# A decoder layer on one core: two kinds of transposes move from the matrix engine to VectorE, DRAM and the DMA queue

## The chip, the core and the metric

The kernel runs on one core of a Trainium2 chip. A core has a matrix engine (PE, whose weight loads are shown as PEld), VectorE (DVE), ScalarE (ACT), GpSimd (POOL) and SyncE (SP), which here only issues transfers. Each engine takes its instructions in order. The metric is the device time of one execution in microseconds (us); a time is a median of several runs.

## What is computed

The input is `x` (32 batches of 128 tokens of 128 channels) and an encoder state `ctx_768` (32 batches of 128 tokens of 96 channels). All is float32. Three blocks follow each other, each of them added to `x`:

```python
x = x + linear_attention(layernorm(x))            # 16 heads of 8, sigmoid q and k
x = x + cross_attention(layernorm(x), ctx_768)    # 16 heads of 64, softmax over 128 encoder tokens
x = x + ffn(layernorm(x))                         # shared SwiGLU + one of 8 experts for each token
```

In the last block, `logits = x3 @ gate_w` with `x3 = layernorm(x)`. The expert is the one with the largest logit; its input is `x3` times the sigmoid of that logit.

## The kernel before

**Groups and pairs.** The 32 batches are 8 groups of 4 (`GT`). Cross-attention is cut into 64 steps: for each group two halves of the heads (`s`), and in each half four batches (`b`). The main loop takes two steps at a time; its variable `a` is 0, 2, ... 62. "Pair 12" in this text is the turn with `a = 12`, that is steps 12 and 13. A group takes eight steps, that is four pairs: 8g, 8g+2, 8g+4 and 8g+6.

**A pair, on PE.** `scores` of both steps; `mix` (tiles `avp`) and `project` (`xyp`) of the two steps before; `queries` (`xqp`); `values` (`vp`); `keys` (`xkp`); and `turn`, which transposes the softmax of the first step (`prTa`, `prTb`), then, after another `keys`, that of the second. Between `scores` and `turn` stands a chain over the other engines: `largest` (DVE, tile `nmax`), `exponentials` (ACT, tile `pr`), `divide` (a reciprocal `rs` on DVE, then a multiplication of `pr` on POOL), and then PE may transpose `pr`.

**Banks.** `bank()` hands out four PSUM buffers in turn. A matmul that takes a buffer waits until the matmul four calls before it has been copied out by DVE or ACT. The helpers `pair()` hand out two larger buffers.

**Work beside the pairs.** Other work is written as generators that stop at named places: `attention(g)`, `prologue(g)` (the second layernorm) and `router(g)` (the third layernorm, logits, the choice of the expert, a token's row in the sorted buffer `xsort`). The loop calls `place("M1")` and so on at fixed places of a pair; every generator that waits at this name goes on to its next stop. `begin` starts them: `attention(a // 8 + 2)` at the end of pairs 2, 10, 18 ... (after it the prologue), `router` of the group just finished in the middle of pairs 10, 18, ... 50, and of group 6 in pair 56. So `router(0)` takes its statistics at the end of pair 10, normalizes in pair 12 (`M1`), is transposed by PE there (`P1`, tile `x3Tp`), copied by ACT to `x3T` (`E2`), has its logits in pair 12 (`P2`, tile `lp`), its maxima in pair 14 (`S1`: five small DVE operations, `top` to `oh`), the scaled rows and the counting in pair 14 (`M1`, `P1`, `E1`: `scored`, `cp`, `placed`) and stores its tokens by indirect transfers in pairs 14 and 16 (`M2`).

**The encoder state.** `load_e(g)` loads four batches, token by token (tile `eg`). PE transposes them in `attention`, behind the matmuls of `oep`, and ACT copies them to `eT`, channels first, as `keys` and `values` need them. Group 0 is done by `encoder`.

**Order.** `InTurn` (line 22) wraps an engine, so that its instructions keep the order in which the program calls them. Transfers of SP are not wrapped: the scheduler puts them where it likes. `clear_sorted(g)` fills the rows of `xsort` of one group with zeros, eight transfers of 264 KB (ten for the last group).

All these instructions are issued by line 40, inside `InTurn`; tiles tell them apart. The lines to know are `load_e` 226, `clear_sorted` 317, `transposed` 383, `attention` 405, `prologue` 560, `queries` 593, `router` 707, and the main loop 1207.

Of the kernel before, what the change touches and what calls it, by code (L numbers as in the profile page):

```python
# [10 lines left out]
F32 = mybir.dt.float32  # L11
I32 = mybir.dt.int32
U32 = mybir.dt.uint32
AF = mybir.ActivationFunctionType
ALU = mybir.AluOpType
AX = mybir.AxisListType

P = 128
# [3 lines left out]
class InTurn:  # L22

    def __init__(self, tc, engine):
        self.tc, self.engine, self.on = tc, engine, False
        self.last, self.transfers = None, []

    def __getattr__(self, name):  # L30
        def issue(*operands, **more):
            transfer = name.endswith("dma_start")
            behind = [] if self.last is None else [self.last]
            if not transfer:
                behind += self.transfers
            with ExitStack() as turn:
                if self.on:
                    for one in behind:
                        turn.enter_context(self.tc.issue_after(one.ins))
                made = getattr(self.engine, name)(*operands, **more)  # L40
            if transfer:
                self.transfers.append(made)
            else:
                self.last, self.transfers = made, []
            return made

        return issue
# [3 lines left out]
def kernel(  # L51
# [31 lines left out]
    nc = tc.nc  # L83
    B, S, D = x.shape
    DE = enc.shape[2]
# [7 lines left out]
    GT = 4  # L93
    NG = B // GT
    GW = GT * S
# [4 lines left out]
    QSCALE = 1.0 / float(DH) ** 0.5  # L100
# [3 lines left out]
    dram = ctx.enter_context(  # L104
        tc.tile_pool(name="dram", bufs=1, space=bass.MemoryType.DRAM)
    )
# [94 lines left out]
    pb = second_part.enter_context(tc.tile_pool(name="pb", bufs=3))  # L201
# [19 lines left out]
    bq_c = column(a_bq, "bq_c", nc.scalar)  # L221


    eg_of = {}

    def load_e(g):
        if g < NG:
            t = pe.tile([P, GT, DE], F32, tag="eg", name=f"eg{g}")
            nc.sync.dma_start(
                out=t, in_=enc[g * GT : (g + 1) * GT].rearrange("b s d -> s b d")  # L230
            )
            eg_of[g] = t
# [84 lines left out]
    def clear_sorted(g):  # L317

        n = GT * S
        first = [e * CAP + g * n for e in range(NE)]  # L320
        if g == NG - 1:
            first += range(NE * CAP, NROW, n)
        for r in first:
            ins = nc.sync.dma_start(
                out=xsort[r : r + n].rearrange("(p k) d -> p k d", p=P), in_=zeros
            )
            for put in sorted_by:
                tc.declare_no_dep(ins.ins, put.ins, reason="those rows lie in front")
            cleared_by.append(ins)

    def unordered(ins, done, why):
# [8 lines left out]
    pe_, dve, act_, pool_ = (  # L340
        InTurn(tc, e) for e in (nc.tensor, nc.vector, nc.scalar, nc.gpsimd)
    )

    def moments(name):
        stats = small.tile([P, GT, 6], F32, tag="stats", name=f"st_{name}")
# [37 lines left out]
    def transposed(src, n, rows, name, ps=None, first=0):  # L383

        ps = bank(name) if ps is None else ps
        for t in range(first, first + n):
            pe_.transpose(ps[0:rows, t * P : (t + 1) * P], src[:, t, :], ident)
        return ps

# [13 lines left out]
    def attention(g, fixed=None):  # L405
# [124 lines left out]
        yield "E3"  # L530
        turned = None
        if g not in eT_of:
            eT_of[g] = pe.tile([DE, GW], F32, tag="eT", name=f"eT{g}")
            turned = act_.copy(eT_of[g], ep[0:DE, :])
            load_e(g + 2)
        ob = pa.tile([P, GT, D], F32, tag="ob", name=f"ob{g}")
        made = dve.tensor_tensor(
            ob, op4, bo_a.unsqueeze(1).to_broadcast([P, GT, D]), ALU.add
# [9 lines left out]


    steps = [(g, s, b) for g in range(NG) for s in range(2) for b in range(GT)]  # L550
    eT_of, xnT_of, qk_of, asked = {}, {}, {}, set()

    def encoder(g, evict):

        eT = pe.tile([DE, GW], F32, tag="eT", name=f"eT{g}")
        eT_of[g] = eT
        evict(eT, transposed(eg_of[g], GT, DE, f"eTp{g}")[0:DE, :])
        load_e(g + 2)

    def prologue(g, fixed=None):  # L560

# [28 lines left out]
        evict(t[:, 1, :], kp)  # L590
        qk_of[g, s, j] = t

    def queries(g, s, j):

        cols = slice((4 * s + j) * P, (4 * s + j + 1) * P)
        asked.add((g, s, j))
        qp = bank(f"xqp{g}_{s}_{j}")
        pe_.matmul(qp, lhsT=wq_x[:, cols], rhs=xnT_of[g], start=True, stop=True)
        act_.activation(qk_of[g, s, j][:, 0, :], qp, AF.Copy, scale=QSCALE)


    v_of, sc_of, pr_of, sums_of, prT_of, oT_of = {}, {}, {}, {}, {}, {}
# [104 lines left out]
    def router(g, part=slice(0, GT)):  # L707
# [4 lines left out]
        of = statistics(xg[g], f"c{name}", part)  # L712
        yield "M1"
        x3 = normalized(xg[g], of, pe, f"c{name}", part)
        yield "P1"
        ps = transposed(x3, n, P, f"x3Tp{name}", first=t0)
        yield "E2"
        if t0 == 0:
            x3T[g] = const.tile([P, GW], F32, tag=f"x3T{g}", name=f"x3T{g}")
        xt = x3T[g]  # L720
        act_.copy(xt[:, t0 * S : (t0 + n) * S], ps[:, t0 * S : (t0 + n) * S])
        yield "P2"
        lp = bank(f"lp{name}")
        for t in range(n):
            pe_.matmul(
# [3 lines left out]
                start=True,  # L729
                stop=True,  # L730
            )
        yield "E3"
        lg = lp[:, 0 : n * NE].rearrange("p (t e) -> p t e", e=NE)
        if n == GT:
            lg = small.tile([P, n, NE], F32, tag="lg", name=f"lg{name}")
# [393 lines left out]
    def place(*which):  # L1129
        for at in which:  # L1130
            for one in list(beside):
                if one[0] == at:
                    one[0] = next(one[1], None)
                    if one[0] is None:
                        beside.remove(one)
                        if one[2] is not None:
                            begin(one[2]())

    for engine in (pe_, dve, act_, pool_):
        engine.on = True

    def whole(g):
# [62 lines left out]
    for a in range(0, n, 2):  # L1207
        both = (a, a + 1)
        scores(a)
        scores(a + 1)  # L1210
        largest(a)
        place("S1")
        if a:
            mix(a - 2)
            mix(a - 1)
        place("S3")
        largest(a + 1)
        exponentials(a)
        for k in both:
            if k + GT < n and steps[k + GT] not in asked:  # L1220
                queries(*steps[k + GT])
        place("M1")
        divide(a)
        if a:
            project(a - 2)
            project(a - 1)

            if a % 8 == 2 and 2 < a < n - 8 or a == n - 8:
                begin(router(steps[a - 1 if a == n - 8 else a - 3][0]))
        for k in both:  # L1230
            if k not in v_of:
                values(k)
        side["now"] = 0
        place("P1")
        if a >= n - 4:
            within["pair"] = 0
            products()
        exponentials(a + 1)
        place("E1")
        divide(a + 1)  # L1240
        place("E2")
        if a == n - 2:
            next(begun[0][1])
        if a == 0:
            for k in (GT + 2, GT + 3):
                queries(*steps[k])
        for k in both:
            if k + GT + 2 < n and steps[k + GT + 2] not in qk_of:
                keys(*steps[k + GT + 2], act_.copy)
            if k == a:  # L1250
                turn(a)
        if a == 0:
            values(2)
        if a == n - 2:
            early = router(NG - 1, slice(0, GT // 2))
            next(early)
            next(early)
        place("S2", "M2")
        side["now"] = 1
        place("P2")  # L1260
        if a >= n - 6:
            within["pair"] = 1
            products()
        place("E3")
        if a == n - 2:
            next(begun[1][1])
            finish()
        while begun and a < n - 2:
            finish()
        turn(a + 1)  # L1270
        if a == 0:
            place("S1")
        if a % 8 == 2:
            clear_sorted(a // 8)
            g = a // 8 + 2
            if g < NG:
                begin(attention(g), lambda g=g: prologue(g))
        if a == 12:
            load_ffn()
        if a == n - 8:  # L1280

            first_part.close()
            pools["g"] = ctx.enter_context(tc.tile_pool(name="pg", bufs=2, side="right"))
            pools["c"] = ctx.enter_context(tc.tile_pool(name="pc", bufs=4, side="right"))
            pd = ctx.enter_context(tc.tile_pool(name="pd", bufs=1, side="right"))
            pools["down"] = pd.tile([P, NE, NC, D], F32, tag="wdr", name="wdr")
            for c in range(NC):
                nc.sync.dma_start(
                    out=pools["down"][:, :, c],
                    in_=rt_down[:, c * P : (c + 1) * P, :].rearrange("e p d -> p e d"),  # L1290
                )
            whole_experts(pd, "up", rt_up)

            pieces += [
                (g, down(g) if c is None else hidden(g, c))
                for g, c in (
                    (0, 0), (0, 1), (1, 0), (1, 1), (2, 0), (2, 1), (0, None),
                    (3, 0), (3, 1), (1, None), (2, None), (3, None),
                )
            ]  # L1300
# [198 lines left out]
```

## Time and profile before

| what | us |
|---|---|
| median of nine runs (lowest, highest) | 621.21 (617.5, 626.33) |
| the profiled execution, its own time | 624.3 |
| its span in the profile | 622.5 |
| PE busy, 4681 matmuls | 598.5 |
| DVE busy | 430.9 |
| ACT busy | 390.3 |
| POOL busy | 248.3 |
| 256 transposes of the softmax's first halves (`prTa`) | 39.2 |
| 28 + 4 transposes of the encoder state (`oep<-ident,eg`, `eTp`) | 4.2 + 0.6 |
| 32 transposes for the router (`x3Tp`) | 5.2 |

The span begins with the first instruction and ends with the last; the execution's own time has 1.8 us more around it. Matmuls are pipelined, so their durations overlap: what one costs PE is the step from its start to the next start, which the timeline shows. The granted clock of the matrix engine is 0.994 over the span. The DMA engines are busy in the first 75 us (loads, and the 66 transfers of `clear_sorted`), and little after that.

### The profile page before, as it was taken

Reading aid. Unit: us, or ns where it says so; the run is one execution under the profiler, and the core shown is the slowest. Engines: PE = TensorE matmul, PEld = TensorE weight load, DVE = VectorE, ACT = ScalarE, POOL = GpSimd, SP = SyncE. Lnnn points to the kernel's source line nnn. Section 1 sums busy time; section 2 is a strip of 40 time slices with the busy share of each in tenths; the row PEclk is TensorE's granted clock in tenths of the full one; section 3 lists DMA queues with packets and bytes.
Section 4 is the critical chain, followed back from the end, with each engine's and each line's share of the span. In section 5 each row is a group of like instructions: output and inputs, shape, how many; then the busy total and the mean of one; then the engine's idle time right before and its main releaser. Section 6 shows DMA issues by size and latency. Waiting matters only on the chain. (4 is left out here: it accounts for less than half of the span.)

```text
span 622.5 us, 13294 instructions
## 1 busy us (share of the span) xinstructions
PE 598.5 (96%) x4681; PEld 451.2 (72%) x4681; DVE 430.9 (69%) x1226; ACT 390.3 (63%) x1414; POOL 248.3 (40%) x248
## 2 busy tenths in 40 slices
PE   8998999999999999999999999999999999997887
PEld 6556777777777777777777767777767766987845
DVE  5747667877786778677867786778657678655435
ACT  4376776776668667766766677677766771544411
POOL 3123423433443444344434453344345344255540
PEclk9989999999999999999999999999999999999989
DMA  6999900000000000000000000013000002342146
GB/s 167 317 363 351 320 2 2 14 2 1 19 14 1 5 28 2 0 12 22 1 2 10 10 2 1 10 57 89 2 10 10 2 9 90 88 109 67 40 117 180
DMA packets 42659, 39.64 MB, mean 64 GB/s; under 512 B 8592, under 2 KB 32656, under 8 KB 42592
## 3 DMA queue, kind: packets, MB, share of 16 engines
q1 hardware_dynamic: 39168, 33.80, 17.7%
q0 software_dynamic: 2144, 4.46, 2.2%
q8 instruction: 38, 0.62, 0.4%
q10 hardware_dynamic: 1280, 0.53, 0.3%
q14 instruction: 29, 0.24, 0.1%
HBM read 14.37 MB, written 24.40 MB: 62 GB/s over the span
## 5 line engine op out<-in xcount | busy, mean ns | idle before, releaser
L40 ACT ACTIVATE pr<-sc,nmax 128x128 f32<-128x128 f32 x512 | 180.5, 387 | 47.7 <-DVE nmax L40 44.9
L40 POOL TENSOR_TENSOR pr<-pr,rs 128x1024 f32<-128x1024 f32 x64 | 121.2, 1897 | 149.3 <-DVE x L40 89.7
L40 ACT ACTIVATION_READ_ACCUMULATOR pr<-sc,nmax 128x1 f32 x512 | 115.8, 226 | 0.0
L40 DVE TENSOR_REDUCE nmax<-sc 128x8 f32<-128x1024 f32 x64 | 78.0, 1220 | 15.2 <-PE sc L40 14.8
L40 PEld LDWEIGHTS xyp<-wo_x,oT 128*128 128x128 f32 x512 | 61.9, 192 | 14.1 <-issue 12.2
L40 PE MATMUL sc<-qk 64*128 64x128 f32 x1024 | 66.0, 279 | 0.7 <-DVE act L40 0.7
L40 PE MATMUL xqp<-xnT_b,wq_x 128*128 128x512 f32 x128 | 64.8, 631 | 0.7 <-ACT xnT_b L40 0.7
L40 PE MATMUL xkp<-eT,wk_x 96*128 96x512 f32 x128 | 65.1, 593 | 0.0
L40 PEld LDWEIGHTS sc<-qk 64*128 64x128 f32 x1024 | 59.9, 187 | 6.7 <-issue 5.0
L40 PE MATMUL avp<-prT,v 128*64 128x128 f32 x1024 | 63.2, 276 | 0.0
L40 PE MATMUL xyp<-wo_x,oT 128*128 128x128 f32 x512 | 62.7, 276 | 0.1
L40 PE MATMUL vp<-wv_x,eT 96*128 96x512 f32 x128 | 60.5, 593 | 0.8 <-ACT qk L40 0.8
L40 PEld LDWEIGHTS avp<-prT,v 128*64 128x64 f32 x1024 | 55.2, 137 | 4.1 <-issue 0.2
L40 DVE COPY prT<-prTa 128x512 f32<-128x512 f32 x64 | 44.0, 687 | 20.0 <-PE prTa L40 19.8
L40 ACT COPY qk<-xkp 128x512 f32<-128x512 f32 x64 | 37.7, 589 | 28.9 <-PE xkp L40 28.4
L40 ACT COPY prT<-prTb 128x512 f32<-128x512 f32 x64 | 37.6, 588 | 28.8 <-PE prTb L40 28.8
L40 DVE COPY v<-vp 128x512 f32<-128x512 f32 x64 | 43.5, 691 | 15.3 <-PE vp L40 15.3
L40 PEld LDWEIGHTS prTa<-ident,pr 128*128 128x128 f32 x256 | 30.4, 141 | 32.0 <-issue 16.4
L40 POOL DMA_INDIRECT ytok<-yt,rows x35 | 34.1, 975 | 36.2 <-DVE rows L40 28.4
L40 DVE COPY oT<-avp 128x512 f32<-128x512 f32 x64 | 42.1, 686 | 5.8 <-PE avp L40 5.8
L40 PE MATMUL rgu<-xT,wt 128*128 128x128 f32 x280 | 37.7, 278 | 6.5 <-ACT xT L40 6.5
L40 PE MATMUL prTa<-ident,pr 128*128 128x128 f32 x256 | 39.2, 275 | 2.6 <-POOL pr L40 2.5
(170 smaller groups left out, 995.6 us busy)
## 6 DMA issues: line engine op xcount, KB each, us to landing
xsort<-zeros SPq DMA_DIRECT2D x66, 264.0 KB
xt<-xsort SPq DMA_DIRECT2D x39, 66.0 KB
yg<-ytok SPq DMA_DIRECT2D x8, 256.0 KB
x<-in_x_dram SPq DMA_DIRECT2D x7, 256.0 KB
out_dram<-x SPq DMA_DIRECT2D x7, 256.0 KB
eg<-in_ctx_dram SPq DMA_DIRECT2D x8, 192.0 KB
wdr<-in_L_ffn_rt_down_dram SPq DMA_DIRECT2D x2, 512.0 KB
up<-in_L_ffn_rt_up_dram SPq DMA_DIRECT2D x1, 1024.0 KB
```

Source lines behind the costliest of these rows:

```text
L40: made = getattr(self.engine, name)(*operands, **more)
```

## The change

Four things are changed.

1. For groups 0 to 5 the router's normalized tokens are transposed without PE. `begin_turning` lets DVE transpose the tile in blocks of 32 x 32 (one operation on 128 x 512) and writes the result to DRAM. `end_turning` reads it back in four transfers whose pieces are 32 elements long, so that the whole is transposed in `x3T`. The logits (`P1`) then come a pair later, and all that follows them too. Groups 6 and 7 are left as they were.
2. The encoder states of groups 2 to 7 are loaded channels first, batch by batch, straight from the input: `load_e(g, b)` reads elements of 4 bytes. The transposes by PE and the copies by ACT remain for groups 0 and 1 alone. `eT` has three buffers.
3. SP's later transfers (`load_e` from group 2 on, `clear_sorted`, both steps of the turning) are put into a fixed order by a strict `InTurn`. `clear_sorted(0)` is called in pair 2, `clear_sorted(1)` in pair 6, `clear_sorted(2)` in pair 14, and so on.
4. In pair 0, DVE and not ACT copies two of the queries. In pair 2, the prologue of group 1 is normalized after `values` and not before `divide`, and transposed at the end of the pair.

```diff
-    def __init__(self, tc, engine):
+    def __init__(self, tc, engine, strict=False):
...
-            transfer = name.endswith("dma_start")
+            transfer = name.endswith("dma_start") and not self.strict
...
+    def load_e(g, b=0):
+        if 2 <= g < NG:
+            if b == 0:
+                t = pe.tile([DE, GT, S], F32, tag="eT", name=f"eT{g}", bufs=3)
+                eT_of[g] = t.rearrange("p b s -> p (b s)")
+            sp_.dma_start(
+                out=eT_of[g][:, b * S : (b + 1) * S],
+                in_=enc[g * GT + b].rearrange("s d -> d s"),
+            )
+        elif g < 2:
...
+    sp_ = InTurn(tc, nc.sync, strict=True)
...
+    def begin_turning(src, name):
+
+        blocks = pb.tile([P, GT * D], F32, tag="oT", name=f"blocks_{name}")
+        dve.transpose(out=blocks, in_=src.rearrange("p t d -> p (t d)"))
+        there = dram.tile([P, GT * D], F32, tag="there", name=f"there_{name}", bufs=2)
+        sp_.dma_start(out=there, in_=blocks)
+        return there
+
+    def end_turning(there, out):
+
+        for j in range(D // 32):
+            sp_.dma_start(
+                out=out[32 * j : 32 * (j + 1), :].rearrange(
+                    "r (t i s) -> r t i s", t=GT, s=32
+                ),
+                in_=there.rearrange("(i r) (t j s) -> j r t i s", r=32, t=GT, s=32)[j],
+            )
...
     def router(g, part=slice(0, GT)):
...
-        yield "P1"
-        ps = transposed(x3, n, P, f"x3Tp{name}", first=t0)
-        yield "E2"
...
-        act_.copy(xt[:, t0 * S : (t0 + n) * S], ps[:, t0 * S : (t0 + n) * S])
-        yield "P2"
+        aside = g < NG - 2
+        if aside:
+            there = begin_turning(x3, f"c{name}")
+            yield "E2"
+            end_turning(there, xt)
+            yield "S2"
+            yield "P1"
+        else:
+            yield "P1"
+            ps = transposed(x3, n, P, f"x3Tp{name}", first=t0)
+            yield "E2"
+            act_.copy(xt[:, t0 * S : (t0 + n) * S], ps[:, t0 * S : (t0 + n) * S])
+            yield "P2"
         lp = bank(f"lp{name}")
...
-        yield "E3"
+        yield "E2" if aside else "E3"
...
-    def queries(g, s, j):
+    def queries(g, s, j, by=None):
...
-        act_.activation(qk_of[g, s, j][:, 0, :], qp, AF.Copy, scale=QSCALE)
+        if by is None:
+            act_.activation(qk_of[g, s, j][:, 0, :], qp, AF.Copy, scale=QSCALE)
+        else:
+            by.tensor_scalar(qk_of[g, s, j][:, 0, :], qp, QSCALE, None, ALU.mult)
...
         for k in both:
             if k + GT < n and steps[k + GT] not in asked:
-                queries(*steps[k + GT])
-        place("M1")
+                queries(*steps[k + GT], by=dve if a == 0 else None)
+
+
+        apart = a == 2
+        if not apart:
+            place("M1")
         divide(a)
...
-        place("P1")
+        if apart:
+            place("M1")
+        else:
+            place("P1")
...
-        place("E2")
+        if not apart:
+            place("E2")
...
+        if apart:
+            place("P1", "E2")
         place("S2", "M2")
...
+        if a > 0:
+            load_e((a - 2) // 8 + 2, (a - 2) % 8 // 2)
+        if a == 2:
+            clear_sorted(0)
+        if a % 8 == 6 and a // 8 + 1 < NG:
+            clear_sorted(a // 8 + 1)
         if a % 8 == 2:
-            clear_sorted(a // 8)
             g = a // 8 + 2
```

More of the change, by code (lines that the diff above doesn't have):

```diff
@@ L22 @@
 class InTurn:
-    def __init__(self, tc, engine):
-        self.tc, self.engine, self.on = tc, engine, False
+    def __init__(self, tc, engine, strict=False):
+        self.tc, self.engine, self.on, self.strict = tc, engine, False, strict
         self.last, self.transfers = None, []
@@ L221 @@
     bq_c = column(a_bq, "bq_c", nc.scalar)
-    eg_of = {}
-    def load_e(g):
-        if g < NG:
+    eg_of, eT_of = {}, {}
+    def load_e(g, b=0):
[8 more added lines that the diff above has]
+        elif g < 2:
             t = pe.tile([P, GT, DE], F32, tag="eg", name=f"eg{g}")
@@ L323, in clear_sorted @@
         for r in first:
-            ins = nc.sync.dma_start(
+            ins = sp_.dma_start(
                 out=xsort[r : r + n].rearrange("(p k) d -> p k d", p=P), in_=zeros
@@ L532, in attention @@
         if g not in eT_of:
-            eT_of[g] = pe.tile([DE, GW], F32, tag="eT", name=f"eT{g}")
+            eT = pe.tile([DE, GT, S], F32, tag="eT", name=f"eT{g}", bufs=3)
+            eT_of[g] = eT.rearrange("p b s -> p (b s)")
             turned = act_.copy(eT_of[g], ep[0:DE, :])
-            load_e(g + 2)
         ob = pa.tile([P, GT, D], F32, tag="ob", name=f"ob{g}")
@@ L550 @@
     steps = [(g, s, b) for g in range(NG) for s in range(2) for b in range(GT)]
-    eT_of, xnT_of, qk_of, asked = {}, {}, {}, set()
+    xnT_of, qk_of, asked = {}, {}, set()
     def encoder(g, evict):
-        eT = pe.tile([DE, GW], F32, tag="eT", name=f"eT{g}")
-        eT_of[g] = eT
+        eT = pe.tile([DE, GT, S], F32, tag="eT", name=f"eT{g}", bufs=3)
+        eT_of[g] = eT = eT.rearrange("p b s -> p (b s)")
         evict(eT, transposed(eg_of[g], GT, DE, f"eTp{g}")[0:DE, :])
-        load_e(g + 2)
     def prologue(g, fixed=None):
@@ L1137, in place @@
                             begin(one[2]())
-    for engine in (pe_, dve, act_, pool_):
+    for engine in (pe_, dve, act_, pool_, sp_):
         engine.on = True
```

## The prediction

> **What bounds the kernel.** I read the engines' shares first, then the idle time of PE by stretches of 20 us, then the timeline of the pairs that the change touches.
>
> ```profile
> PE 598.5 (96%) x4681; PEld 451.2 (72%) x4681; DVE 430.9 (69%) x1226; ACT 390.3 (63%) x1414; POOL 248.3 (40%) x248
> ```
>
> PE is busy for 96% of the span. In the stretches from 80 to 430 us it is never idle for more than 0.04 us in 20. So work taken from PE there counts in full, as long as nothing else becomes late. What can be late is the chain between scores and transposes: `nmax` (DVE), exponentials (ACT), `rs` (DVE), `pr` (POOL). I measured it in every pair from the timeline: end of POOL's `pr` against the start of PE's `prTa`. Pair 12, where `router(0)` and `attention(3)` meet, has sc at 123.20. PE, then DVE, then POOL:
>
> ```profile
> 130.68 1.88 PE L40 MATMUL vp<-wv_x,eT 96*128 96x512 f32 x4
> 132.40 0.60 PE L40 MATMUL x3Tp<-ident,xn_c 128*128 128x128 f32 x4
> 132.84 0.60 PE L40 MATMUL xnTp_a<-ident,xn_a 128*128 128x128 f32 x4
> 133.28 1.02 PE L40 MATMUL xkp<-eT,wk_x 96*128 96x512 f32 x2
> 134.14 0.60 PE L40 MATMUL prTa<-ident,pr 128*128 128x128 f32 x4
> ...
> 135.88 0.95 PE L40 MATMUL lp<-gw_f,x3T 128*128 128x8 f32 x8
> ```
> ```profile
> 129.67 1.11 DVE L40 TENSOR_SCALAR xn_c<-x,mv_c,rstd_c 128x128 f32<-128x128 f32 x4
> 130.68 1.12 DVE L40 TENSOR_SCALAR xn_a<-x,mv_a,rstd_a 128x128 f32<-128x128 f32 x4
> 131.71 0.21 DVE L40 RECIPROCAL rs<-sums 128x8 f32<-128x8 f32 x1
> ```
> ```profile
> 132.09 3.75 POOL L40 TENSOR_TENSOR pr<-pr,rs 128x1024 f32<-128x1024 f32 x2 [3.56 <-DVE x L40]
> ```
>
> PE's step for four transposes is 132.84 - 132.40 = 0.44 us. The first `pr` ends at about 133.97 and PE takes it at 134.14: 0.17 us to spare. DVE has no gap before `rs`, so whatever is added to DVE there moves `pr`.
>
> **What leaves PE.** Router: 6 x 0.44. Encoder: 6 x 0.44. Together 5.3 us, if PE finds nothing late. ACT's twelve copies (0.59 each) go too, but ACT bounds none of the pairs concerned.
>
> **Pairs 12, 20, 28, 36, 44.** In the order of the changed program DVE's block transpose stands between `xn_c` and `xn_a`, ahead of `rs`. It is in no row of the trace. Nearest rows, 128 x 512 float32 from SBUF to SBUF: `x<-ob,x` 0.69; below it twice the copy `wt<-up` of 128 x 256, 0.60; above it the reduction of 128 x 1024, 1.22. It can't be below zero, since it is added. I take 0.7, the row of its own size. `pr` is then ready at 10.77 + 0.70 + 0.05 = 11.52 us after sc. PE, without `x3Tp`, comes at 10.94 - 0.44 = 10.50 and waits 1.02. `lp` (0.81, from 135.88 to 136.69, where `kvp` starts) leaves this pair. Sum: -0.44 - 0.81 + 1.02 = **-0.23** a pair.
>
> **Pairs 14, 22, 30, 38, 46.** `lp` comes (0.81), `cp` goes (0.36: 149.53 to 149.89). DVE loses `top` to `oh`, `scored` and `placed`, so nothing gets late: **+0.45**.
>
> **Pairs 16, 24, 32, 40, 48.** Here `attention` has its second statistics, and the router's `top` to `oh` (142.67 to 143.66, 0.99) and `scored` (146.06 to 147.08, 1.02) now come on top. The pair before the change, sc at 155.50:
>
> ```profile
> 159.84 1.28 DVE L40 COPY oT<-avp 128x512 f32<-128x512 f32 x2
> 161.04 1.22 DVE L40 TENSOR_REDUCE nmax<-sc 128x8 f32<-128x1024 f32 x1
> 162.17 1.11 DVE L40 TENSOR_SCALAR xn_n<-att,mv_n,rstd_n 128x128 f32<-128x128 f32 x4
> 163.19 0.20 DVE L40 RECIPROCAL rs<-sums 128x8 f32<-128x8 f32 x1
> 163.30 0.44 DVE L40 TENSOR_TENSOR x<-xyp,x 128x128 f32<-128x128 f32 x2
> ```
> ```profile
> 161.23 1.95 PE L40 MATMUL xyp<-wo_x,oT 128*128 128x128 f32 x16
> 163.02 1.88 PE L40 MATMUL vp<-wv_x,eT 96*128 96x512 f32 x4
> 164.74 1.02 PE L40 MATMUL hlp<-xnT_a,wh_a 128*128 128x512 f32 x2
> ```
>
> The first `oT` ends 0.99 later, 6.02 after sc; PE wants it at 5.73: about 0.4 of waiting. Then `cp` needs the bank of the first `xyp`, which DVE frees with `x<-xyp,x`: at 7.80 + 0.24 + 0.99 + 1.02 + 0.1 = 10.15. PE comes there at 9.24 + 0.4 = 9.64: another 0.5. Behind these 0.9 us both `pr` are ready in time (11.99 against 12.7; about 15.08 against 15.30). With `cp` in (0.36) and the encoder's transposes out (0.44): 0.9 + 0.36 - 0.44 = **+0.82**.
>
> So a full group costs -0.23 + 0.45 + 0.82 = +1.04; five groups **+5.2**. The new waits eat the saving: they come to 1.02 + 0.9 a group against 0.88 of transposes.
>
> **The rest of the loop.** Pair 8 has encoder transposes but no router: -0.44, cover 2.2. `router(5)` has no `attention` beside it. In pair 52 the second `prTa` can't come before 12.33 after sc, the time set by exponentials alone in pairs 10, 18, 26; it came at 13.05: -0.7. In pair 54 PE waits 1.24 because `placed` delays `rs`:
>
> ```profile
> 456.59 0.66 PE L40 MATMUL prTa<-ident,pr 128*128 128x128 f32 x4 [1.24 <-POOL pr L40]
> ```
>
> That goes (-1.15 with `lp` in and `cp` out) and comes back in pair 56 (+1.3). Together -0.55; all three -1.0.
>
> **First pairs.** Pair 0: PE idles 0.77 (0.93 with the lag) ahead of a `vp` whose bank ACT frees after 16 exponentials; two copies (0.6 each) go to DVE, idle there for 2.4 us, and ACT is 0.96 earlier: -0.9. Pair 2: the second `pr` now follows its exponentials at once, `prTa` at 11.9 and not 12.22: -0.3. Together **-1.2** (bounds -2.6, all idle time of both pairs, and 0).
>
> **Transfers.** SP executes in order: write of blocks, four reads, two loads, eight clears, two loads. Each load has 96 x 128 pieces of 4 bytes, 768 for each of 16 DMA engines. Columns of 4-byte pieces (8.6 to 9.4 us) and a load of 384-byte pieces (110 to 111.25) give prices (packets, MB, share of the 16 engines' time):
>
> ```profile
> q1 hardware_dynamic: 207, 0.00, 12.0%
> ```
> ```profile
> q1 hardware_dynamic: 527, 0.20, 63.4%
> ```
>
> 0.120 x 16 x 0.8 us / 207 = 7.4 ns; 0.634 x 16 x 1.25 / 527 = 24 ns. At 7.4 a load takes 5.7 us, at 24 it takes 18.4. In the cycle of pair 12 blocks leave at 131.5, and reads land by about 137 (each way some 2.1 us, as the load of 109.07 took). Logits want them at 149.6: 12 us to spare. Three loads and the clears (54 us for 66, so 6.5 for 8) must land before `keys` at 180.6: 3T + 6.5 < 43.5, so T < 12.3 us, or 16 ns a piece. I take 7.4, the row with the same bytes: **0**.
>
> The Trainium skill ("DMA: Bandwidth & Descriptors", Rules for kernel authors) says that a strided last dimension becomes one descriptor per element, and "VectorE: DVE Perf Modes" (The three transpose paths) that such a copy is 19 times slower than the crossbar's 1309 ns for 128 x 128 bf16. An estimate from that page is 19 x 1.309 x 96 / 128 = 18.7 us a load, past the 12.3; the sum would be that of the second rival. The 4-byte row speaks against it; no row has this stride.
>
> **Sum.** +5.2 - 1.0 - 1.2 = +3.0 us on the profiled execution: 624.3 becomes 627.3. The median shown is 621.21, 3.1 below it; I give the forecast on the median's scale: 624.2. Range of this case: with 0.60 for the block transpose -0.5, with 1.22 +2.6; first pairs -1.4 to +1.2; with some noise of the median, 620 to 629.5.
>
> **Rivals.**
> 1. *The cover holds.* If PE's order, not DVE's chain, decides (slack is larger than I read, or DVE's small operations fit gaps), only PE's work counts: -5.3 - 1.2 = 614.7. For it: PE showed no wait in these pairs. Against it: 0.17 us of slack and a DVE row without gaps. Chance 0.30.
> 2. *Loads come late* (slower). It decides from 12.3 us a load in the queue that carries everything. At 24 ns, 137.1 + 6.5 + 55.2 = 198.8 against 180.6: PE stands 18 us ahead of `keys` in each of groups 3 to 7, +91: 715. For it: 24 ns at 384 bytes. Against it: 7.4 ns at 4 bytes. Chance 0.15.
> 3. Forecast: chance 0.55, the gain eaten by DVE.
>
> Half a per cent (3.1 us: 618.1 to 624.3) is about what a measurement of this kernel tells from no change. The forecast's case lies on that border: 0.28 within, 0.27 above. The first rival gives 0.29 faster, 0.01 same; the second 0.15 slower. Faster 0.29, same 0.29, slower 0.42. The range must reach the first rival and leaves out the second: 613.5 to 629.5.
>
> **What would show it.** Right: in pairs 12, 20 ... 44 an idle PE of about 1.0 before the first `prTa`, released by POOL's `pr`; in pairs 16 ... 48 waits before `xyp` (DVE `oT`) and `cp` (DVE `x`), 0.9 in all; those three pairs 47.7 long before, 48.8 after; loads of about 6 us. Wrong: no waits there (rival 1), or PE idle ahead of `xkp` or `lp`, released by a DMA (rival 2), or a block transpose far from 0.7 us.

## The result and the profile after

The changed kernel takes 624.97 us (median of 20 runs, 623.34 to 630.16); the kernel before 619.68 us (median of 62 runs). The ratio is 1.0085, 95% interval 1.0069 to 1.0102: 5.3 us slower. The forecast was slower by 3.0 us.

The profiled executions differ by 2.4 us only (626.7 against 624.3). The loop shows why that number is too small. From the first `sc` to the last pair's `sc` it takes 462.47 us before (36.95 to 499.42) and 468.28 after (36.94 to 505.22): +5.81. Behind the last `sc`, where the experts are, the same work took 123.1 and 119.7 us; in all kernels of this study 117 to 123, in no order that follows the edits: in the kernel of experiment 5, which leaves that part as it was before, 119.7. So kernels are compared below by the loop and its pairs, and by ratios of medians.

First the engines' shares of the changed kernel, to be read against the line of before: TensorE has 48 instructions and 1.9 us less, VectorE 8.2 us more.

```profile
PE 596.6 (95%) x4633; PEld 444.7 (71%) x4633; DVE 439.1 (70%) x1234; ACT 381.7 (61%) x1400; POOL 249.0 (40%) x248
```

TensorE's waits from 80 to 430 us (waited for, us in total, times, longest). The kernel before has no entry in this view; now there are two, each five times, once a group:

```profile
PE prTa L40 <- POOL pr L40: 4.2, 5, 1.1
PE cp L40 <- DVE x L40: 1.9, 5, 0.7
```

Pair 12 (sc at 121.74), from the timelines of VectorE, GpSimd and TensorE:

```profile
128.22 1.11 DVE L40 TENSOR_SCALAR xn_c<-x,mv_c,rstd_c 128x128 f32<-128x128 f32 x4
129.36 0.71 DVE L40 STREAM_TRANSPOSE blocks_c<-xn_c 128x512 f32<-128x512 f32 x1
129.99 1.08 DVE L40 TENSOR_SCALAR xn_a<-x,mv_a,rstd_a 128x128 f32<-128x128 f32 x4
130.97 0.20 DVE L40 RECIPROCAL rs<-sums 128x8 f32<-128x8 f32 x1
```
```profile
131.35 3.75 POOL L40 TENSOR_TENSOR pr<-pr,rs 128x1024 f32<-128x1024 f32 x2 [4.28 <-DVE x L40]
```
```profile
130.95 0.60 PE L40 MATMUL xnTp_a<-ident,xn_a 128*128 128x128 f32 x4
131.39 1.12 PE L40 MATMUL xkp<-eT,wk_x 96*128 96x512 f32 x2
133.30 0.66 PE L40 MATMUL prTa<-ident,pr 128*128 128x128 f32 x4 [0.78 <-POOL pr L40]
```

`x3Tp` is gone from TensorE, and VectorE's block transpose stands where there was no gap: `rs` comes 9.23 after sc instead of 8.51, `pr` as much later. From `xkp` to `prTa` it is 1.91 us where a step of two `xkp` is 0.86 (134.14 - 133.28 before): 1.05 of waiting, of which the view lists 0.78. The listed idle time begins at the modelled end of a matmul; the distance from start to start is the better measure.

Pair 16 (sc at 154.27), VectorE and TensorE:

```profile
156.69 0.18 DVE L40 TENSOR_REDUCE top<-lg 128x4 f32<-128x32 f32 x1
...
159.48 1.29 DVE L40 COPY oT<-avp 128x512 f32<-128x512 f32 x2
160.68 1.22 DVE L40 TENSOR_REDUCE nmax<-sc 128x8 f32<-128x1024 f32 x1
...
162.22 0.69 DVE L40 TENSOR_TENSOR xs<-xn_c,score 128x512 f32<-128x512 f32 x1
162.83 1.11 DVE L40 TENSOR_SCALAR xn_n<-att,mv_n,rstd_n 128x128 f32<-128x128 f32 x4
163.85 0.20 DVE L40 RECIPROCAL rs<-sums 128x8 f32<-128x8 f32 x1
163.96 0.44 DVE L40 TENSOR_TENSOR x<-xyp,x 128x128 f32<-128x128 f32 x2
```
```profile
160.23 2.05 PE L40 MATMUL xyp<-wo_x,oT 128*128 128x128 f32 x16
162.11 1.88 PE L40 MATMUL vp<-wv_x,eT 96*128 96x512 f32 x4
164.26 0.41 PE L40 MATMUL cp<-oh,behind 128*128 128x32 f32 x2 [0.27 <-DVE x L40]
164.51 0.39 PE L40 MATMUL cp<-oh,onesP 128*128 128x32 f32 x2
164.73 1.10 PE L40 MATMUL hlp<-xnT_a,wh_a 128*128 128x512 f32 x2
```

`top` to `oh` ahead of the statistics, and the scores ahead of `xn_n`, make `rs` come 9.58 after sc (7.69 before). `xyp` starts 0.23 later after sc than before, `cp` 0.43 later than `vp`'s step of 1.72 allows; the steps of `xyp`, `cp` and `hlp` (the matmul of `attention` that follows) are 0.28 longer in all. With `cp` in and the encoder's transposes out, the pair is 16.30 us long instead of 15.43. Only the wait ahead of `cp` is in the list of waits; the lateness of `xyp` shows in its start alone.

The lone channels-first load of the changed kernel (issued at 88.07) in the transfers of 87 to 97 us: busy tenths in 40 slices, then packets, MB and share of 16 engines.

```profile
DMA  0000000049995686999999999999999988000000
...
q1 hardware_dynamic: 12304, 0.05, 87.3%
```

Its packets run from 89.05 to 95.39: 6.3 us, 7.3 from issue, for 768 pieces a DMA engine: 8.2 ns a piece.

Length of the pairs, us, before and after, beside what the forecast gave:

| pairs | before | after | change in all | forecast |
|---|---|---|---|---|
| 0, 2 | 13.70, 13.24 | 12.70, 13.23 | -1.0 | -1.2 |
| 8 | 15.42 | 14.99 | -0.4 | -0.4 |
| 12, 20, 28, 36, 44 | 17.12 to 17.38 | 16.90, 17.13 to 17.46 | 0.0 | -1.15 |
| 14, 22 ... 46 | 15.18 | 15.63 | +2.2 | +2.25 |
| 16, 24 ... 48 | 15.43 | 16.30 to 16.72 | +4.9 | +4.1 |
| 18, 26 ... 50 | 13.35 | 13.35 to 13.47 | +0.4 | 0 |
| 52, 54, 56 | 42.08 | 41.95 | -0.1 | -0.55 |
| 58 | 14.27 | 14.16 | -0.1 | 0 |

### The profile page after: what moved, and what is told of

It reads as the page before. It is cut to its first block, busy times and chain, and to the rows that moved or that the text cites. A ratio compares the mean times of both kernels' runs of the same rounds, so it can differ in the third digit from the quotient of the medians.

```text
span 624.9 us, 13285 instructions
## 1 busy us (share of the span) xinstructions
PE 596.6 (95%) x4633; PEld 444.7 (71%) x4633; DVE 439.1 (70%) x1234; ACT 381.7 (61%) x1400; POOL 249.0 (40%) x248
## 3 DMA queue, kind: packets, MB, share of 16 engines
q1 hardware_dynamic: 344832, 36.95, 58.2%
## 5 line engine op out<-in xcount | busy, mean ns | idle before, releaser
L40 PEld LDWEIGHTS xyp<-wo_x,oT 128*128 128x128 f32 x512 | 61.4, 192 | 16.2 <-issue 7.9
L40 DVE COPY oT<-avp 128x512 f32<-128x512 f32 x64 | 42.2, 687 | 11.4 <-PE avp L40 11.1
```

## Experiments

The theory: TensorE loses 5.3 us of work, and VectorE's chains to `prTa` and to `cp`, made longer by the block transpose and by the router's small operations, put more than that back as waits. The rivals: the length is set by something else (the way through DRAM, the loads' queue, contention).

**1. The block transpose behind `rs`.**

```diff
         if aside:
+            yield "E1"
             there = begin_turning(x3, f"c{name}")
```

> The block transpose of groups 0 to 5 is issued on VectorE behind the first reciprocal of its pair instead of ahead of it; nothing else changes. Theory (VectorE's chain to the first prTa decides): in pairs 12, 20, 28, 36, 44 the idle PE before the first prTa (0.78 to 1.09 us in the changed kernel) goes, these pairs take 15.9 to 16.2 us instead of 16.9 to 17.5, pair 52 loses 0.4 more; pairs 16 to 48 stay at 16.3 to 16.7. Sum about -4.5 us against the changed kernel, ratio to the kernel before 1.001. Rival (the length of these pairs is set by something else, the longer way through DRAM among it): pairs 12 to 44 stay at 16.9 to 17.5, ratio 1.0085.

Measured: 1.0027 (0.9995 to 1.0059); loop 465.02, 3.26 shorter than in the changed kernel. Pairs 12 to 44 take 16.19, 16.51, 16.40, 16.75, 16.42; their reciprocal is back at 8.52 in pair 12. VectorE and TensorE in pair 12 of this kernel (sc at 120.52):

```profile
128.02 1.12 DVE L40 TENSOR_SCALAR xn_a<-x,mv_a,rstd_a 128x128 f32<-128x128 f32 x4
129.04 0.20 DVE L40 RECIPROCAL rs<-sums 128x8 f32<-128x8 f32 x1
...
130.70 0.71 DVE L40 STREAM_TRANSPOSE blocks_c<-xn_c 128x512 f32<-128x512 f32 x1
```
```profile
130.17 1.02 PE L40 MATMUL xkp<-eT,wk_x 96*128 96x512 f32 x2
131.37 0.66 PE L40 MATMUL prTa<-ident,pr 128*128 128x128 f32 x4 [0.17 <-POOL pr L40]
```

The wait falls from 0.78 to 0.17 and the pair by 0.71, the transpose's duration. The theory holds. Pairs 20 to 44 are longer than the expected 15.9 to 16.2 (experiment 7 shows why they differ from pair 12), and the sum was 1.2 short: `prTa` still waits a little, since TensorE comes 0.44 earlier against 0.17 to spare, and pair 52 became 0.33 longer (it was to lose 0.4): there the transpose delays the second `rs` to 10.64.

**2. The router's small operations out of the full pair.**

```diff
-        yield "S1"
+        yield "S2" if aside else "S1"
         top = small.tile(...)
...
-        if n == GT:
+        if n == GT and not aside:
             yield "M1"
             scored()
...
         placed(cp)
+        if aside:
+            yield "S2"
+            scored()
```

> The router's top to oh go from the pair with attention's second statistics (16, 24 ...) into the pair before it, and its scores to the end of the pair; the block transpose stays ahead of the reciprocal. Theory (these small VectorE operations delay oT and x<-xyp and so PE's xyp and cp): pairs 16 to 48 take 15.35 us (15.43 of before, + 0.36 for cp, - 0.44 for the encoder's transposes) instead of 16.3 to 16.7, unless the second prTa is late behind the placing, which I price at 0 to 0.4; pairs 12 to 44 keep their wait. Sum about -4.5 us, ratio to the kernel before 1.001. Rival (cp's place ahead of hlp costs this by itself, or the pairs are long for contention with the loads): pairs 16 to 48 stay above 16.0, ratio 1.0085.

Measured: 1.0011 (0.9976 to 1.0046); loop 463.24, 5.04 shorter. Pairs 16 to 48 take 15.43 or 15.44, where 15.35 was expected; `cp` waits for nothing, though it stands ahead of `hlp` as in the changed kernel. Pairs 12 to 44 keep their wait of 0.76 to 0.78.

**3. Both.** The two edits above in one kernel.

> Both edits together. Theory: the two waits are independent and both go; only PE's work is left, so the loop is 9 to 10 us shorter than the changed kernel's and some 4 us shorter than that of the kernel before: ratio to the kernel before 0.992 to 0.995. Rival (DRAM round trip or loads are next to be late, or the second prTa is): ratio 0.998 to 1.004, with idle PE before lp, xkp or the second prTa.

Measured: 0.9958 (0.9932 to 0.9984); loop 460.00, 8.28 shorter than in the changed kernel (3.26 + 5.04 = 8.30: the two waits add up) and 2.47 shorter than before. It is faster than the kernel before, by less than was expected (9 to 10 us of loop, 0.992 to 0.995): pairs 20 to 44 still take 16.50 to 16.52, with TensorE waiting 2.2 us before `prTa` in the five full pairs.

**4. Loads and first pairs without the router's new way.**

```diff
-        aside = g < NG - 2
+        aside = False
```

> The changed kernel with its router as before (transposes on TensorE, logits in the same pair); the channels-first loads, the fixed order of SyncE and the new first pairs stay. Theory (the loads cost nothing and take 0.44 us of TensorE's time out of six pairs; the first pairs give 1.0): -2.6 - 1.0 = -3.6 us, ratio to the kernel before 0.994; pairs 16 to 48 at 15.0 us, pairs 12, 14, 20, 22 as before. Rival (the loads' queue or their contention costs something of the changed kernel's 5 us): pairs longer than before, ratio 0.998 to 1.004.

Measured: 0.9955 (0.9928 to 0.9983); loop 458.57, 3.90 shorter than before. Pairs 16 to 48 take 14.99 each; pairs 12, 14, 20, 22 are as before to 0.01. The loads cost nothing here and give their 0.44 in six pairs. The loss of the changed kernel is the router's.

**5. The first pairs alone.** The kernel before with these lines:

```diff
-                queries(*steps[k + GT])
-        place("M1")
+                queries(*steps[k + GT], by=dve if a == 0 else None)
+        apart = a == 2
+        if not apart:
+            place("M1")
```

the parameter `by` of `queries` as in the change and, in pair 2 alone, the prologue's M1 behind the values and P1, E2 at the end of the pair.

> The kernel before with the changed kernel's pairs 0 and 2 alone (two queries evicted by VectorE, the prologue of group 1 around the second half of pair 2). Theory: pair 0 takes 12.7 us instead of 13.7, pair 2 stays at 13.2, all else as before: -1.0 us, ratio to the kernel before 0.998. Rival (what pair 0 gains is given back in pairs 2 to 6): ratio 1.000, pairs 2 to 6 together 1 us longer.

Measured: 0.9967 (0.9939 to 0.9995); loop 461.41, 1.06 shorter. Pair 0 takes 12.71, pair 2 13.22. Nothing is given back.

**6. The router's new way without the loads.** Encoder states in one load a group, transposed by TensorE as before.

```diff
-        if 2 <= g < NG:
+        if 2 <= g < 0:
...
-        elif g < 2:
+        elif g < NG and b == 0:
```

> The changed kernel with the encoder states loaded and transposed by TensorE as before the change; router, first pairs and SyncE's order stay. Theory (the loads cost no time and take 0.44 us out of pairs 8, 16 ... 48; the 0.4 us that pair 32 has more than pairs 24 and 40 is an instruction fetch made slow by a load): pair 8 takes 15.4 us, 16 to 48 take 16.7 to 16.8, pair 32 too; pairs 20 to 44 keep 17.1 to 17.5 and 26 to 50 their 13.4 (these come from GpSimd's puts). The loop is 2 us longer than the changed kernel's: ratio to the kernel before 1.011 to 1.013. Rival (traffic of the loads stretches the pairs): pairs 20 to 50 get shorter than in the changed kernel, ratio 1.007 or below.

Measured: 1.0157 (1.0098 to 1.0215), where 1.011 to 1.013 was expected; loop 470.85, 2.57 longer than in the changed kernel (some 2 expected). Pairs 16 to 48 are 16.73 to 16.80, pair 32 17.16. So one half of what I expected of pair 32 is wrong: its stall is there without any load. VectorE at that place in this kernel:

```profile
286.61 0.18 DVE L40 RECIPROCAL score<-en 128x4 f32<-128x4 f32 x1
287.17 0.17 DVE L40 COPY xs<-tokno 128x4 f32<-128x4 f32 x1 [0.38 <-issue]
```

The changed kernel shows the same 0.38 ahead of the same instruction, where VectorE waited for nothing that the profile shows. In the kernels of experiments 2, 3 and 8, whose VectorE has another order, it is not there. What it is stays open; a load is not its cause. Pairs 26 to 50, on the other hand, are 13.35 here and not 13.45. That does not show that a load's packets cost the 0.1: in experiment 2, which has the loads, the same pairs take 13.32 or 13.33, and in the changed kernel pair 50 is long (13.45), though no packet moves in the 6 us ahead of it (415 to 421.4; the last load was issued at 405.74). GpSimd and VectorE there (sc at 421.47):

```profile
421.75 1.21 POOL L40 DMA_INDIRECT xsort<-xs,row  x1 [0.30 <-issue]
```
```profile
423.20 1.23 DVE L40 TENSOR_REDUCE nmax<-sc 128x8 f32<-128x1024 f32 x1 [0.47 <-PE sc L40]
```

In experiment 6 the put (an indirect transfer of GpSimd) of this pair starts 0.16 ahead of sc and not 0.28 behind it, and `nmax` starts 1.35 after sc and not 1.73. So the 0.1 goes with where the put stands, as far as the runs tell; in pair 18 of the changed kernel, where it starts 0.42 behind sc, nothing is late.

**7. The second half of the rows put earlier.**

```diff
-                yield "M2"
+                yield "S2" if aside and t else "M2"
             put = pool_.indirect_dma_start(
```

> The changed kernel; only the second half of the rows of groups 0 to 4 is put by GpSimd ahead of the next router's reciprocal root instead of behind it. Theory (the 0.3 us by which oT and all after it are late in pairs 20, 28, 36, 44, but not in 12, comes from GpSimd's indirect transfers at that moment): these pairs fall from 17.13 to 17.46 us to 16.9 as pair 12, the first reciprocal to 9.25 after sc. Rival (it comes from the loads or from instruction fetches, or the put only shifts it): they stay at 17.1 to 17.5.

Measured in the profile (a single run): pairs 20, 28, 44 take 16.90 or 16.91, pair 36 17.21 instead of 17.46 (it is 0.25 longer than the others before the change too, which stays open); pair 52 takes 13.35 instead of 13.61; loop 466.75, 1.53 shorter. GpSimd and VectorE in pair 20 of the changed kernel (sc at 183.92), whose indirect transfers are the puts:

```profile
185.49 1.06 POOL L40 DMA_INDIRECT xsort<-xs,row  x1 [0.18 <-issue]
186.85 0.96 POOL L40 DMA_INDIRECT xsort<-xs,row  x1 [0.30 <-issue]
```
```profile
187.98 0.17 DVE L40 TENSOR_SCALAR var_a<-mv_a 128x4 f32<-128x4 f32 x1
188.37 1.29 DVE L40 COPY oT<-avp 128x512 f32<-128x512 f32 x2 [0.22 <-PE avp L40]
```

and VectorE at the same place with the puts 1.25 us earlier after sc (sc at 184.10):

```profile
188.16 0.17 DVE L40 TENSOR_SCALAR var_a<-mv_a 128x4 f32<-128x4 f32 x1
188.24 1.28 DVE L40 COPY oT<-avp 128x512 f32<-128x512 f32 x2
```

`oT` starts 0.08 behind `var_a`, not 0.39. The 0.3 belongs to where the puts stand, and so does the 0.26 of pair 52. The releaser named, `avp`, had started all its matmuls by 187.8 in either kernel, as in pair 12, where `oT` waits for nothing; in what way a put holds VectorE is open. Pairs 26 to 50 take 13.38 to 13.40; in pair 26 their put still starts 0.28 after sc.

**8. A version without the waits.** Both edits; besides, the router's normalization too behind `rs`, the puts as in 7, and the router of group 5 on TensorE.

```diff
-        yield "M1"
+        aside = g < NG - 3
+        yield "E1" if aside else "M1"
         x3 = normalized(xg[g], of, pe, f"c{name}", part)
```

> Both edits, and more: the router's normalization goes behind the reciprocal with the block transpose, the second half of the rows is put ahead of the next router's statistics, and the router of group 5 stays on TensorE as before the change. Theory: no wait is left in the full groups, pairs 12 to 44 take 15.9 us, 14 to 46 15.6, 16 to 48 15.4, 18 to 50 13.35: 60.3 a group against 61.1 before the change; with the first pairs and the group 8 to 10 the loop is 5 to 6 us shorter than the one before: ratio to the kernel before 0.991 to 0.993. Rival (VectorE's work merely moves the wait to the second prTa or to the logits): pairs 12 to 44 at 16.2 or more, ratio 0.995 or above.

Measured: 0.9894 (0.9877 to 0.9910), 610.89 us against 617.29 of the kernel before beside it; loop 456.23, 6.24 shorter than before. A group takes 15.80 + 15.63 + 15.43 + 13.33 = 60.19 us, 0.89 less than the 61.08 of before: the two transposes' 0.88. TensorE in pair 12 of this kernel:

```profile
131.02 0.60 PE L40 MATMUL xnTp_a<-ident,xn_a 128*128 128x128 f32 x4
131.46 1.02 PE L40 MATMUL xkp<-eT,wk_x 96*128 96x512 f32 x2
132.32 0.60 PE L40 MATMUL prTa<-ident,pr 128*128 128x128 f32 x4
```

From `xkp` to `prTa` 0.86, no wait. This beats both kernels: what is taken off TensorE is gained once VectorE's chain lets it. The gain is a little above what I expected (0.991 to 0.993; 5 to 6 us of loop, 6.24 measured).

**9. The block transpose twice.**

```diff
         dve.transpose(out=blocks, in_=src.rearrange("p t d -> p (t d)"))
+        dve.transpose(out=blocks, in_=src.rearrange("p t d -> p (t d)"))
```

> The block transpose is issued twice, the second time into the same tile. Theory (it stands ahead of the reciprocal on a full engine and the first prTa waits for that): each of pairs 12 to 44 is 0.6 to 0.7 us longer, 17.5 to 18.1, their wait 1.4 to 1.8; pair 52 0.5 to 0.7 longer; sum 3.5 to 4 us of loop. Rival (cover somewhere): no pair longer by over 0.2.

Measured in the profile (a single run): pair 12 17.65 (+0.75), pairs 20 to 44 17.83 to 18.17 (+0.68 to +0.73), pair 52 +0.67; loop +3.86. The listed wait before `prTa` stays at 0.79 in pair 12, where 1.4 to 1.8 was expected; the rest shows in `xnTp_a`, because `xn_a` is late as well (1.03 us from its start to `xkp`, 0.44 without the edit). What is added to VectorE ahead of `rs` here, TensorE loses.

**10. Every channels-first load twice.**

```diff
             sp_.dma_start(
                 out=eT_of[g][:, b * S : (b + 1) * S],
                 in_=enc[g * GT + b].rearrange("s d -> d s"),
             )
+            sp_.dma_start(
+                out=eT_of[g][:, b * S : (b + 1) * S],
+                in_=enc[g * GT + b].rearrange("s d -> d s"),
+            )
```

> Every channels-first load is issued twice, into the same place; the result is the same. Theory (from the times of the changed kernel's packets a load takes some 10 us of all 16 engines, and the queue has 61 us for four loads, the clears and the blocks): with some 20 us for a pair of loads a group needs 4 x 20 + 8 = 88 us of queue for 61 us of work, so TensorE waits for eT or x3T by a DMA in groups 3 to 7, in all 90 to 130 us: 715 to 755 us. Rival (the loads' time is latency, or lies beside other work however long): within 1% of the changed kernel, 619 to 631 us.

Measured (a single run): 693.11 us. TensorE's waits from 80 to 500 us:

```profile
PE xkp L40 <- DMA eT<-in_ctx_dram: 43.0, 4, 11.4
PE xkp L40 <- issue: 10.4, 1, 10.4
```

and SyncE's queue (start, time until the last was issued, how many):

```profile
133.23 25.59 SPq L40 DMA_DIRECT2D eT<-in_ctx_dram  x4
158.87 11.40 SPq L40 DMA_DIRECT2D xsort<-zeros  x8
170.31 27.10 SPq L40 DMA_DIRECT2D eT<-in_ctx_dram  x4
```

The cover ends where loads become too long, as the second rival of the prediction said; it is no latency hidden without limit. But it is 68 us and not 90 to 130: I had taken the price of a load from the packets' summed time (10 us), and packets overlap (from 88 to 96 us of the changed kernel their share of 16 engines is 109.2%). A full queue issues four loads in 25.6 or 27.1 us: 6.4 to 6.8 us a load. Eight clears take 11.4 us of it, not the 6.5 of the prediction.

## Why the prediction was right, step by step

The direction, the mechanism and its three places were right; the size was 2.8 us too small on the loop (+3.0 forecast, +5.8 measured). That the time of 624.2 came so close to the median of 624.97 is in part luck: the kernel before has a median of 619.68 over 62 runs, 1.5 below the 621.21 from which I counted. The 2.8 are 1.1 in pairs 12 to 44, 0.8 in 16 to 48, 0.4 in 18 to 50, 0.4 in 52 to 56, 0.2 in the first pairs, less 0.1 in pair 58.

- **TensorE's work.** 12 x 0.44: confirmed by pair 8 (-0.43) and by experiment 4 (0.44 in each of six pairs).
- **Block transpose.** Forecast 0.7 from `x<-ob,x`, measured 0.71. Wait of 1.02 forecast in pair 12, 1.05 by the starts; pair 12 -0.23 forecast, -0.22 measured. Experiments 1 and 9 show cause and price.
- **Pairs 14 to 46.** +0.45 forecast, +0.44 to +0.45 measured.
- **Pairs 16 to 48.** +0.82 forecast, +0.87 and +0.88 in pairs 16 and 24, +1.30 in pair 32, +0.93 and +0.92 in 40 and 48; experiment 2 takes it all away. The parts agree less than their sum: I had 0.4 of waiting before `xyp` and 0.5 before `cp`, the lines of pair 16 give 0.23 and 0.43, and slower steps, which I did not have, give 0.28. The 0.42 in pair 32 is the stall of experiment 6.
- **The step that was mis-sized** is "pairs 12, 20, 28, 36, 44": I took pair 12 for all five. In the other four the puts of the group before, which the change moves into them a pair later, add 0.23 to 0.31: +1.0 in all (experiment 7). I had let the puts move with the rest of the router at no price. Another 0.4 came in pairs 26 to 50, where a put starts shortly behind sc; a load's packets are not needed for it (pair 50, experiment 6), but how the put makes `nmax` late is not shown.
- **Group 5.** Pair 52 -0.44 for -0.7: the missing 0.26 is the puts of group 4, which I had not put there; with them earlier it takes 13.35, -0.70 (experiment 7). Pair 54 -1.01 for -1.15, 56 +1.32 for +1.3. The wait behind `placed` went from pair 54 to pair 56 with its length, 1.24.
- **First pairs.** Pair 0 -1.0 for -0.9. Pair 2 0.0 for -0.3: its first `prTa` came 1.2 earlier, but the second half's reciprocal stayed at 9.88 after sc, set by the exponentials, and the second `prTa` at 12.21.
- **Transfers.** 0, and 0 measured. The time T of a load was forecast at 5.7 us; alone it is 6.3, in a full queue 6.4 to 6.8. The bound of 12.3 had the clears at 6.5; with 11.4 it is 10.7, and was not reached either. The 4-byte row was the right one. The Trainium skill's 19 times for a transpose by strides ("VectorE: DVE Perf Modes", The three transpose paths) gave an estimate of 18.7 us: three times what was measured here, for float32 and 12,288 pieces. The page says it for a large innermost stride of the destination; here the destination's innermost elements lie side by side and the source is strided, so the estimate went beyond the page. That each element becomes its own piece ("DMA: Bandwidth & Descriptors", Rules for kernel authors) is what the trace shows: 12,304 packets for 12,288 elements.
- **Rival 1** (only TensorE's work counts, 614.7) fell; it had -6.5 us against the median of before, and experiment 8 reaches -6.4 (610.89 against 617.29) once the chains are cleared. **Rival 2** (loads late) fell at this size and came at twice the size.

## What to carry to other kernels

Taking work off the bounding engine pays only if what replaces it isn't put ahead of that engine's releaser on another full engine: find the instruction that releases it (here `rs`), and issue new work behind it. Nearly the same operations cost 5.8 us of loop in one order and gained 6.2 in another (experiment 8, which leaves group 5's router on TensorE). Price every repetition of a pattern, not the first alone: what a moved stage issues last (here GpSimd's puts) lands in the next repetition.

## What was not expected of the hardware

- GpSimd's indirect transfers of 128 rows delayed VectorE by 0.3 us where they ended shortly ahead of a copy from PSUM, with no dependency between the two that the profile shows (experiment 7). In pairs 26 to 50 a put that started 0.28 us behind sc was recorded with 1.21 us, one that started 0.16 ahead of it with 0.96, and VectorE's next reduction came 0.4 us later beside the first, also where no load was in flight (pair 50, experiment 6).
- Summed packet times overstate a queue of small pieces: a lone load of 6.3 us shows as 8.7 us of 16 engines (87.3% of a window of 10 us).
